# Who makes the rounding additions behind the loop of a cross-attention and feed-forward layer: VectorE or ScalarE

## The chip, the cores and the metric

The kernel runs on one core of one Trainium2 chip. The metric is the device time of one execution in microseconds (us). Three executions of the kernel before took 684.77, 685.49 and 688.87 us; their median, 685.49 us, is the time that the change is set against.

## What is computed

The layer takes 2048 tokens of 256 features. Cross-attention is followed by a feed-forward part with 1024 hidden features, whose two products use weights and activations that are rounded to few levels:

```python
def act_quant(x):
    scale = 127.0 / jnp.clip(jnp.max(jnp.abs(x), axis=-1, keepdims=True), 1e-05)
    return jnp.clip(jnp.round(x * scale), -128, 127) / scale
...
h = bit_linear(x, w1)                  # x rounded by act_quant, w1 to -1, 0, 1
h = depthwise_conv1d(h.transpose(0, 2, 1), conv_w, conv_b)   # three taps along the tokens
h = silu(h.transpose(0, 2, 1))
return bit_linear(h, w2)               # h rounded by act_quant again
```

and outside it `x = x + attention(...)`, then `x = x + feed_forward(layernorm(x))`. So activations are rounded twice: once each block of 128 tokens before the first product, and once the 1024 hidden features of each token before the second. The kernel rounds by adding 12582912 (`MAGIC`) in float32 and taking it away again: behind the first addition only whole numbers fit.

## The kernel before, in words

**The loop.** Attention is done in 8 units (4 stretches of 512 query tokens by 2 pairs of heads), each over all blocks of 128 keys. While units of one stretch run, the feed-forward of earlier tokens is woven in by a plan of calls (`at`, `plan`). Feed-forward works on groups of 256 tokens, `g` = 0 to 7, and in each on 4 slots of 256 hidden features (`NP` = 4): slot `s` belongs to group `s // 4`. Groups 0 to 3 and the first slot of group 4 are computed in the loop, but group 3's rounding and second product are left over.

**Behind the loop** come the last attention rows (four blocks of 128 tokens, `NQB - NSUB` onwards, that is 12 to 15) and 15 slots of groups 4 to 7. Their order is written by hand: `for i in range(N + 4): head(i); tick(i)`, and then one call of `rest` (what group 3 still owes: `scales_spread`, `rounding` of half 0, `rounding` of half 1, and two `end_product`, one for each tick from tick 1 on). Every instruction is kept in program order on its engine, so each engine works through its own list and an instruction that waits holds up all behind it on that engine.

`head(i)`, for i = 1 to 4, finishes block i - 1: normalised tokens `y`, their largest magnitude, the scale `qsc`, then the steps of `quantize` (line 760): `y` times the scale, then the two additions of `MAGIC` in one instruction into the bf16 tile `yq`. TURN (line 765), at the end of a tick, transposes `yq` on TensorE, and ScalarE copies it into `xq_all`.

`tick(i)` (line 1150) moves several slots on by one step each:

- ScalarE: `end_silu` of slot i - 2 (its odd half, from `pre`) and of slot i - 1 (its even half, from the PSUM tile `ph`), lines 904 to 912; both write into the tile `t` of the group.
- VectorE: `dequantize` of slot i (`h` from `ph`, line 822); `output` of products of the tick before (`res`, line 965); `end_last_tap` (line 895).
- ScalarE: `end_taps` of slot i (`pre` and `side`, line 874).
- TensorE: `hidden` of slot i + 1 into one of two `ph` banks (line 811), which the even `end_silu` of slot i - 1 has to have read, then the convolution `end_convolve` of slot i (line 887).

In four of a group's ticks something more is done, at numbers 4, 6, 7 and 8 of the dictionary `at_`: at 4 `magnitudes` of the first four hidden chunks (half 0), at 6 those of half 1, then `columns` and `scales` (the token scales: a transpose, a maximum, a reciprocal, and `cm` on GpSimd); at 7 `scales_spread` (transposes, then ScalarE copies them into `tb`) and `rounding` of half 0; at 8 `rounding` of half 1 and, at the end of the tick, both products `py` of the group. The tick after that is number 5 of the next group, and its `output` calls wait for the products. So a group takes four ticks, and number 8 of one group is number 4 of the next. For the last group, 7, the numbers come one tick later, and its rounding is done in four pieces of 128 tokens at the end.

`rounding(g, i)` (line 945) takes half i of a group (256 tokens by 4 chunks, 1024 elements in each partition): VectorE multiplies `t` by `tb` in place, then makes both additions in one instruction from `t` into the bf16 tile `hq`. The product (line 957) reads all of `hq` as weights: 8 matmuls for each of two blocks of 128 tokens, the first four of each from half 0.

Two buffers matter: `ph` has two banks behind the loop (`ps_h`), and `hq` has one buffer.

Of the kernel before, what the change touches and what calls it, by code (L numbers as in the profile page):

```python
# [10 lines left out]
F32 = mybir.dt.float32  # L11
BF16 = mybir.dt.bfloat16
I32 = mybir.dt.int32
U8 = mybir.dt.uint8
AF = mybir.ActivationFunctionType
ALU = mybir.AluOpType
# [3 lines left out]
P = 128  # L20
FMAX = 3.4028234663852886e38
MAGIC = 12582912.0
# [7 lines left out]
def layer(  # L30
# [22 lines left out]
    nc = tc.nc  # L53

    _, NL, D = x.shape
# [7 lines left out]
    NQB = NL // P  # L63
    G = 256
    QPG = G // P
    NG = NL // G
    QW = 512
    NU = NL // QW
    NSUB = QW // P
# [13 lines left out]
    const = ctx.enter_context(tc.tile_pool(name="const", bufs=1))  # L83
# [9 lines left out]
    ones16 = const.tile([P, P], BF16, name="ones16")  # L93
    nc.vector.memset(ones16, 1.0)

    neg_half = const.tile([P, 2 * H], F32, name="neg_half")
    nc.gpsimd.memset(neg_half, -0.5)

    def inverse_root(x, floor, op, rows, shape, gpsimd=nc.gpsimd):

        gpsimd.tensor_scalar(x, x, floor, None, op)
        e = neg_half[:rows, : shape[-1]] if len(shape) == 1 else neg_half[
            :rows, : shape[0] * shape[1]
        ].rearrange("p (a b) -> p a b", a=shape[0])
        gpsimd.tensor_tensor(x, x, e, ALU.pow)
# [47 lines left out]
    def big(name):  # L153
        return ps_b.tile([P, 2, 512], F32, tag="big", name=name)

    def bank(name, shape, dtype=F32):
        return ps_1.tile(shape, dtype, tag="bank", name=name)
# [16 lines left out]
    tensor, vector = InOrder(nc.tensor), InOrder(nc.vector)  # L174
    scalar, gpsimd = InOrder(nc.scalar), InOrder(nc.gpsimd)
# [108 lines left out]
    with tc.tile_pool(name="pro", bufs=1, side="right") as pro, tc.tile_pool(  # L284
        name="pw", bufs=2, side="right"
# [244 lines left out]
        if NLK == 1:  # L530
            box = {}
# [66 lines left out]
    def quant_scales(amax, n, vector=nc.vector):  # L598

        vector.tensor_scalar(amax, amax, QUANT_EPS, 1.0 / 127.0, ALU.max, ALU.mult)  # L600
        sc = sm.tile([P, QPG], F32, tag="qsc", name="qsc")
        vector.reciprocal(sc[:, :n], amax)
        return sc

    def product_units(amax, i):

        vector.tensor_scalar(amax, amax, w_mean[:, i : i + 1], None, ALU.mult)

    def as_rows(cols, n, by_scalar=False):

        cm = sm.tile([P, QPG, P], F32, tag="cm", name="cm", bufs=3)
        for i in range(n):
            if by_scalar:
                scalar.activation(cm[:, i, :], ones, AF.Copy, scale=cols[:, i : i + 1])
            else:
                gpsimd.tensor_scalar(cm[:, i, :], ones, cols[:, i : i + 1], None, ALU.mult)
        return cm
# [7 lines left out]
    wk = ctx.enter_context(tc.tile_pool(name="wk", bufs=1, side="right"))  # L625
# [3 lines left out]
    with att:  # L629
# [99 lines left out]
        def block_steps(qb, oT, sub, po):  # L729
            box = {}  # L730

            def project_out():
                box["po"] = po()
                for c in range(ND):
                    tensor.matmul(
                        box["po"], oT[:, c, ts(sub, P)], wo_sb[:, c, :],
                        start=(c == 0), stop=(c == ND - 1),
                    )

            def residual():  # L740
                vector.tensor_tensor(x1[qb], box["po"], x1[qb], ALU.add)
                st = sm.tile([P, 6], F32, tag="st3", name="st3")
                box["mv"] = sm.tile([P, 2], F32, tag="mv3", name="mv3")
                vector.bn_stats(st, x1[qb])
                vector.bn_aggr(box["mv"], st)

            def inverse_deviation():
                inverse_root(box["mv"][:, 1:2], LN_EPS, ALU.add, P, (1,), gpsimd)

            def normalize():  # L750
                box["y"] = wk.tile([P, D], F32, tag="y", name="y")
                vector.tensor_scalar(
                    box["y"], x1[qb], box["mv"][:, 0:1], box["mv"][:, 1:2], ALU.subtract, ALU.mult
                )
                vector.tensor_reduce(
                    units1[:, qb : qb + 1], box["y"], AX.X, ALU.max, apply_absolute_value=True
                )
                box["sc"] = quant_scales(units1[:, qb : qb + 1], 1, vector)

            def quantize():  # L760
                vector.tensor_scalar(box["y"], box["y"], box["sc"][:, 0:1], None, ALU.mult)
                box["yq"] = wk.tile([P, D], BF16, tag="yq", name="yq", bufs=2)
                vector.tensor_scalar(box["yq"], box["y"], MAGIC, -MAGIC, ALU.add, ALU.add)

            def transpose():

                t0 = OFF + qb * P
                tp = bank("tpy", [P, 2, P])
                yT = tp[:, 0, :].bitcast(BF16).rearrange("p (c t) -> p c t", c=ND)
                for c in range(ND):  # L770
                    tensor.transpose(yT[:, c, :], box["yq"][:, ts(c, P)], ident16)
                tensor.transpose(tp[:, 1, :], box["cm"][:, 0, :], ident)
                scalar.copy(xq_all[:, :, t0 : t0 + P], yT)
                scalar.copy(ib_all[:, 1 + qb * P : 1 + (qb + 1) * P], tp[:, 1, :])

            def bias():
                gpsimd.tensor_tensor(x1[qb], x1[qb], bo_sb, ALU.add)

            def unit_row():
                product_units(units1[:, qb : qb + 1], 0)  # L780
                box["cm"] = as_rows(units1[:, qb : qb + 1], 1)

            return (
                bias, project_out, residual, inverse_deviation, normalize, quantize, unit_row,
                transpose,
            )
# [12 lines left out]
        for edge in (0, NL + 1):  # L799
# [3 lines left out]
        NC2 = NH // 2  # L803
        groups_ = [{} for _ in range(NG)]
        chunk = {}
        where = {
            "ph": big, "py": lambda: big("py")[:, 0, :D], "later": False,
            "t": lambda: fp.tile([P, G, NC2], F32, tag="t", name="t", bufs=3),
        }
# [135 lines left out]
        def rounding(g, i, tokens=slice(0, G)):  # L945
            b = groups_[g]
            t = b["t"][i][:, tokens, :]
            vector.tensor_tensor(
                t, t, b["tb"][:, tokens].unsqueeze(2).to_broadcast(list(t.shape)), ALU.mult
            )  # L950
            if "hq" not in b:
                b["hq"] = fp.tile([P, G, NH], BF16, tag="hq", name="hq", bufs=1)
            vector.tensor_scalar(
                b["hq"][:, tokens, ts(i, NC2)], t, MAGIC, -MAGIC, ALU.add, ALU.add
            )

        def product(g, i):
            b = groups_[g]
# [23 lines left out]
        def feed_forward(g, k, slots, pace=2):  # L982

            for n in range(slots):
                s, t = g * NP + n, k + n * pace
                for m, call in (
                    (-1, hidden), (-1, dequantize), (0, taps), (1, last_tap), (3, silu),
                ):
                    at(t + m, lambda call=call, s=s: call(s), LATE)
                if n % 2:  # L990
                    at(t + 4, lambda n=n: magnitudes(g, n // 2), LATE)
            if slots < NP:
                return
            t = k + NP * pace
            for m, call in (
                (3, columns), (3, scales), (5, scales_spread), (5, lambda g: rounding(g, 0)),
                (6, lambda g: rounding(g, 1)), (7, lambda g: end_product(g, 0)),
                (7, lambda g: end_product(g, 1)),
            ):
                at(t + m, lambda call=call: call(g), LATE)  # L1000
# [8 lines left out]
        def unit_beat(k):  # L1009

            u, b = divmod(k, NB)
            return (u, b, beats[b]) if u < len(units) else (u, b, [])
# [11 lines left out]
        for k in range(len(units) * NB):  # L1024
            u, b, blocks = unit_beat(k)
            v, _, following = unit_beat(k + 1)
            g, pr = units[u]
# [55 lines left out]
        def y_bank(name):  # L1083
# [5 lines left out]
            later=True,  # L1089
            t=lambda: ptp.tile([P, 2, QW], F32, tag="pt", name="t").rearrange(  # L1090
                "p h q -> p (h q)"
            ).rearrange("p (t c) -> p t c", c=NC2),
# [13 lines left out]
        def po(sub):  # L1106
            if sub % 2 == 0:
                pos[sub // 2] = y_bank("po")
            return pos[sub // 2][:, ts(sub % 2, D)]
# [40 lines left out]
        def tick(i):  # L1150
# [23 lines left out]
            if 7 in at_ and at_[7] != NG - 1:  # L1174
                scales_spread(at_[7])
                rounding(at_[7], 0)
# [76 lines left out]
```

## Time and profile before

The profile is of one execution of 688.55 us. Its traced span is 686.7 us, which leaves 1.85 us around it. The loop ends at about 591 us; the part behind it is what the change touches.

| | before |
|---|---|
| median of three runs | 684.77 / 685.49 / 688.87 us (lowest, median, highest) |
| profiled execution, its span | 688.55 us, 686.7 us |
| mean granted clock of TensorE | 0.972 |
| busy in the span | PE 629.2, VectorE (DVE) 464.1, ScalarE (ACT) 423.8, GpSimd (POOL) 276.6 us |
| 594.5 to 686.8 us, behind the loop | PE 57.67, DVE 74.03, ACT 35.85, POOL 26.78 us of 92.3 us |

The timeline view has a line for each instruction, or for some alike in a row: start, duration, engine, line, operation, tile written and tiles read, sizes, count; in brackets the idle time of the engine just before, and what ended it. All engine calls behind the loop go through a helper at line 170, so lines are told apart by their tiles: `hq<-t` is the rounding of hidden features, `yq<-y` that of a block. A view of stretches gives for each stretch of time the busy time of every engine with the number of instructions, then the granted clock of TensorE (1.00 is full speed), the share of the DMA engines and GB/s. A view of groups adds up instructions of one kind: busy us and mean ns of one, then the idle time before them.

### The profile page before, as it was taken

What the parts mean: (1) busy time and instruction counts of PE and PEld (TensorE: products, weight loads), DVE (VectorE), ACT (ScalarE), POOL (GpSimd) and SP (SyncE); (2) the same over time, 40 slices, a digit from 0 to 9 for tenths busy, and PEclk for the clock granted to TensorE, in tenths of its full rate; (3) what the DMA queues carried; (4) which work ended last, traced back from release to release, by engine and by line L of the source; (5) the groups of instructions that cost most, each with busy time, mean ns of one, the idle gap of its engine ahead of it and who ended that gap; (6) DMA issues with size and microseconds to landing.
All of it is one profiled execution on the core that took longest, in us unless ns stands there. A gap on an engine that the chain in (4) does not pass through costs nothing. (4 is left out here: it accounts for less than half of the span.)

```text
span 686.7 us, 8000 instructions
## 1 busy us (share of the span) xinstructions
PE 629.2 (92%) x2796; PEld 266.3 (39%) x2796; DVE 464.1 (68%) x770; ACT 423.8 (62%) x535; POOL 276.6 (40%) x331
## 2 busy tenths in 40 slices
PE   4999898999999999999999999998899999857754
PEld 2555563333333333333334333332333333345542
DVE  3658774332832766596378779757966797897885
ACT  1656556554556445669945469998765789545540
POOL 2656673221221234244245433425354446742330
PEclk9999999999999999999999999999999999997975
DMA  7600003685878674478849447693564576100001
GB/s 241 170 0 0 1 1 92 128 161 111 167 140 183 128 148 93 93 154 152 185 96 172 101 107 154 125 182 94 107 123 92 132 138 114 31 0 16 16 16 36
DMA packets 32220, 72.12 MB, mean 105 GB/s; under 512 B 7531, under 2 KB 16940, under 8 KB 32172
## 3 DMA queue, kind: packets, MB, share of 16 engines
q0 software_dynamic: 16560, 60.30, 43.3%
q1 hardware_dynamic: 14524, 10.45, 5.1%
q10 hardware_dynamic: 1088, 0.79, 0.4%
q8 instruction: 24, 0.39, 0.2%
q14 instruction: 24, 0.20, 0.1%
HBM read 9.13 MB, written 2.10 MB: 16 GB/s over the span
## 5 line engine op out<-in xcount | busy, mean ns | idle before, releaser
L170 ACT ACTIVATE pt<-st,bias 128x1024 f32<-128x1024 f32 x232 | 242.8, 1112 | 123.1 <-issue 64.6
L170 PE MATMUL st<-q_un,kT 64*128 64x512 f32 x928 | 223.7, 611 | 4.7 <-DVE res L170 1.8
L170 PE MATMUL ot<-pt,v_sb 128*64 128x512 f32 x928 | 216.6, 600 | 0.0
L170 DVE TENSOR_TENSOR vec<-vec,pt 128x1024 f32<-128x1024 f32 x107 | 136.7, 1278 | 40.2 <-ACT pt L170 36.3
L170 PEld LDWEIGHTS st<-q_un,kT 64*128 64x128 f32 x928 | 83.0, 187 | 124.8 <-issue 91.3
L170 PEld LDWEIGHTS ot<-pt,v_sb 128*64 128x64 f32 x928 | 60.2, 136 | 136.7 <-issue 130.4
L170 POOL DMA_DIRECT2D acd<-pt x54 | 44.9, 831 | 127.9 <-ACT pt L170 61.4
L170 POOL DMA_DIRECT2D acc<-pt x61 | 52.7, 865 | 69.4 <-ACT pt L170 51.7
L170 POOL TENSOR_TENSOR pre<-pre,side 128x512 f32<-128x512 f32 (+1 forms) x32 | 38.3, 1196 | 62.3 <-DVE pre L170 51.4
L170 ACT ACT_TABLE_LOAD x34 | 43.6, 1283 | 16.6 <-DMA lb<-in_L_xattn_ln_l_b_dram 7.4
L170 PE MATMUL kv<-wkv_sb,feat 128*128 128x512 f32 (+1 forms) x116 | 52.9, 599 | 0.0
L170 POOL TENSOR_TENSOR ss<-ss,neg_half 128x8 f32<-128x8 f32 (+1 forms) x23 | 39.1, 1702 | 1.9
L170 ACT ACTIVATE t<-pre 128x512 f32<-128x512 f32 (+1 forms) x32 | 29.7, 928 | 11.8 <-POOL pre L170 11.6
L170 POOL TENSOR_SCALAR cm<-ones,units 128x128 f32<-128x128 f32 x16 | 11.8, 739 | 61.4 <-DVE units L170 57.9
L170 DVE COPY oT<-ot 128x512 f32<-128x512 f32 x8 | 5.5, 691 | 44.6 <-PE ot L170 44.6
L170 DVE TENSOR_REDUCE ss<-sq 128x8 f32<-128x512 f32 (+1 forms) x23 | 15.5, 672 | 29.0 <-ACT sq L170 28.9
L170 DVE TENSOR_TENSOR h<-ph,ib_all 128x516 f32<-128x516 f32 x32 | 21.9, 686 | 19.0 <-PE ph L170 18.6
L170 PE MATMUL ph<-h,dg 128*128 128x256 f32 x90 | 25.8, 428 | 7.4 <-DVE h L170 7.4
L170 DVE RECIPROCAL r<-dn 128x512 f32<-128x512 f32 (+1 forms) x11 | 27.3, 2478 | 5.7 <-PE dn L170 5.7
L170 PEld LDWEIGHTS kv<-wkv_sb,feat 128*128 128x128 f32 (+1 forms) x116 | 21.2, 192 | 21.9 <-issue 20.9
L170 ACT ACTIVATE side<-h,cw_sb 128x256 f32<-128x256 f32 x66 | 29.6, 506 | 0.0
L170 PE MATMUL py<-w2T,hq 128*128 128x256 bf16 x128 | 20.8, 317 | 7.2 <-DVE hq L170 7.2
(129 smaller groups left out, 708.9 us busy)
## 6 DMA issues: line engine op xcount, KB each, us to landing
acc<-pt POOLq DMA_DIRECT2D x61, 512.0 KB, 5.1
acd<-pt POOLq DMA_DIRECT2D x54, 512.0 KB, 4.8
tok<-in_x_dram SPq DMA_DIRECT2D x4, 512.0 KB, 6.1
w_sb<-in_L_ffn_w_dram SPq DMA_DIRECT2D x4, 512.0 KB, 5.3
q_un<-in_x_dram SPq DMA_DIRECT2D x4, 512.0 KB, 3.9
out_dram<-res SPq DMA_DIRECT2D x16, 128.0 KB, 1.7
tok<-in_ctx_dram SPq DMA_DIRECT2D x3, 512.0 KB, 4.7
wkv_sb<-in_L_xattn_W_kv_dram ACTq DMA_DIRECT2D x1, 512.0 KB, 7.2
```

The costliest lines, as they stand in the source:

```text
L170: return tc.keep_in_program_order(getattr(self.engine, name)(*args, **kwargs))
```

## The change

Two constants, `MAGIC` and `-MAGIC`, are put into a tile of two columns, and the additions move to ScalarE, each as an activation with the function Identity and one column as its bias. For the last four blocks the multiplication by the scale is taken into the first activation. For hidden features VectorE keeps the multiplication, and the additions of all groups whose rounding stands behind the loop (3, 4, 5 and 6) are made by ScalarE; group 7 and all rounding inside the loop stay as they were. Nothing else is moved: on TensorE, GpSimd and the DMA queues the order of instructions is the same; on ScalarE the new instructions stand where the calls stand.

```diff
+    magic = const.tile([P, 2], F32, name="magic")
+    nc.vector.memset(magic[:, 0:1], MAGIC)
+    nc.vector.memset(magic[:, 1:2], -MAGIC)
...
             def quantize():
+                box["yq"] = wk.tile([P, D], BF16, tag="yq", name="yq", bufs=2)
+                if qb >= NQB - NSUB:
+                    scalar.activation(
+                        box["y"], box["y"], AF.Identity, bias=magic[:, 0:1], scale=box["sc"][:, 0:1]
+                    )
+                    scalar.activation(box["yq"], box["y"], AF.Identity, bias=magic[:, 1:2])
+                    return
                 vector.tensor_scalar(box["y"], box["y"], box["sc"][:, 0:1], None, ALU.mult)
-                box["yq"] = wk.tile([P, D], BF16, tag="yq", name="yq", bufs=2)
                 vector.tensor_scalar(box["yq"], box["y"], MAGIC, -MAGIC, ALU.add, ALU.add)
...
-            vector.tensor_scalar(
-                b["hq"][:, tokens, ts(i, NC2)], t, MAGIC, -MAGIC, ALU.add, ALU.add
-            )
+            hq = b["hq"][:, tokens, ts(i, NC2)]
+            if where["later"] and g < NG - 1:
+                scalar.activation(t, t, AF.Identity, bias=magic[:, 0:1])
+                scalar.activation(hq, t, AF.Identity, bias=magic[:, 1:2])
+            else:
+                vector.tensor_scalar(hq, t, MAGIC, -MAGIC, ALU.add, ALU.add)
```

## The prediction, as it was made before the changed kernel ran

> **What bounds the kernel now.** I read the stretches behind the loop first, cut at the start of one `h` in each group, then the groups of instructions there, and last the timelines of VectorE, ScalarE and TensorE in one group. The stretches:
>
> ```profile
> core 0: us, PE busy (x) PEld busy (x) DVE busy (x) ACT busy (x) POOL busy (x), PEclk, DMA share, GB/s
> 595.30:610.10 14.80, 9.70 (x49) 6.65 (x48) 13.02 (x34) 4.66 (x10) 5.53 (x10) 1.00 0.00 1
> 610.10:623.60 13.50, 6.38 (x29) 4.12 (x28) 12.81 (x30) 5.59 (x13) 5.11 (x8) 0.80 0.00 0
> 623.60:639.10 15.50, 13.41 (x72) 10.54 (x72) 12.43 (x19) 8.87 (x19) 4.94 (x6) 0.85 0.06 18
> 639.10:653.68 14.58, 10.43 (x62) 7.92 (x61) 12.82 (x22) 8.79 (x17) 5.21 (x6) 1.00 0.05 19
> ```
>
> VectorE is busy 12.8 of 14.58 us in the undisturbed group (fourth row), ScalarE 8.8. At first sight VectorE is the bound and ScalarE has 5.8 us to spare. But ScalarE's spare time is not free: it sits in the chain. The timeline of VectorE in that group:
>
> ```profile
> 647.40 1.22 DVE L170 TENSOR_TENSOR t<-t,tb 128x1024 f32<-128x1024 f32 x1 [1.29 <-ACT tb L170]
> 648.66 0.69 DVE L170 TENSOR_SCALAR hq<-t 128x1024 bf16<-128x1024 f32 x1
> 649.27 0.69 DVE L170 TENSOR_TENSOR h<-ph,ib_all 128x516 f32<-128x516 f32 x1
> 649.88 0.47 DVE L170 SCALAR_TENSOR_TENSOR pre<-h,cw_sb,pre 128x256 f32<-128x256 f32 x1
> 650.27 1.22 DVE L170 TENSOR_TENSOR t<-t,tb 128x1024 f32<-128x1024 f32 x1
> 651.52 1.11 DVE L170 TENSOR_SCALAR hq<-t 128x1024 bf16<-128x1024 f32 x1
> 652.55 1.21 DVE L170 TENSOR_REDUCE m<-t 128x256 f32<-128x1024 f32 x1
> 653.68 0.68 DVE L170 TENSOR_TENSOR h<-ph,ib_all 128x516 f32<-128x516 f32 x1
> 654.28 0.86 DVE L170 SCALAR_TENSOR_TENSOR res<-py,am,q_un 128x256 f32<-128x256 f32 x2
> ```
>
> From the first multiplication of `t` to the end of both `res` VectorE runs without a wait, 7.66 us (the next instruction starts at 655.06). ScalarE and TensorE beside it:
>
> ```profile
> 647.27 0.68 ACT L170 ACTIVATE t<-pre 128x256 f32<-128x256 f32 x1
> 648.67 0.73 ACT L170 ACTIVATE t<-ph,cb_sb 128x256 f32<-128x256 f32 x1 [0.72 <-PE ph L170]
> ```
>
> ```profile
> 649.44 0.60 PE L170 MATMUL ph<-xq_all,w1T 128*128 128x258 bf16 x4 [0.82 <-ACT t L170]
> 650.02 1.56 PE L170 MATMUL ph<-h,dg 128*128 128x256 f32 x6
> 651.41 0.60 PE L170 MATMUL py<-w2T,hq 128*128 128x256 bf16 x4
> 652.69 1.53 PE L170 MATMUL py<-w2T,hq 128*128 128x256 bf16 x12 [0.67 <-DVE hq L170]
> ```
>
> The reader is to see who waits for whom: the even silu (`t<-ph`) frees a bank for `hidden`; `hidden` gives the next `h`; the last 12 matmuls of `py` start when the second `hq` is there; `res` needs them. Now they are just done before VectorE comes to them.
>
> **What leaves VectorE.** Eight `hq` of 1024 elements take 0.61 or 1.02 us each until the next instruction starts (648.66 to 649.27, 651.52 to 652.55), four of each kind: about 6.5 us. Four blocks shed `y` times scale and `yq`, 602.81 to 603.41 = 0.60 each: 2.4 us. In all 8.9 us of 74. Two memsets of one column join VectorE at the start, near the row `second` (0.06 us), while it waits 4.33 us for the first tokens: nothing.
>
> **What ScalarE gets.** Sixteen activations of 1024 and eight of 256 elements. The trace has no Identity of 1024; the nearest row is the exponential of the same size with a bias column:
>
> ```profile
> L170 ACT ACTIVATE pt<-st,bias 128x1024 f32<-128x1024 f32 x232 | 242.8, 1112 | 123.1 <-issue 64.6
> ```
>
> and, of the groups behind the loop, two of 256 elements and the instruction that is replaced:
>
> ```profile
> L170 ACT ACTIVATE pre<-h,cb_sb,cw_sb 128x256 f32<-128x256 f32 x15 | 8.8, 588 | 20.1 <-DVE h L170 20.1
> L170 ACT ACTIVATE side<-h,cw_sb 128x256 f32<-128x256 f32 x15 | 7.4, 495 | 0.0
> L170 DVE TENSOR_SCALAR hq<-t 128x1024 bf16<-128x1024 f32 x8 | 7.2, 898 | 0.3
> ```
>
> By length the exponential is nearest: I take 1.11 us, with 0.95 as the lower end (a tile in SBUF with one column less) and 1.30 as the upper (silu writes `t` with gaps and takes 0.68 where `side` takes 0.49, so the gaps in `hq` might add 0.19). The second activation needs the first's result, so nothing overlaps: 1.11 + 0.04 + 1.11 = 2.26 us a pair, against 0.69 to 1.10 for one instruction before. The 256-wide pair is `pre`'s 0.60 plus `side`'s 0.49. No table load is added: Identity (`pre`) and Silu alternate behind the loop, and the last load there stands at 590.56.
>
> Here a rule speaks against the change: the Trainium skill, "ScalarE: Activation LUTs", section "Rules for kernel authors", puts plain additions on VectorE, not on ScalarE. The row agrees in price (2.26 against about 0.9), but price alone would make the change good or bad by which engine has time: by busy sums the group would have VectorE 12.8 - 1.6 = 11.2 and ScalarE 8.8 + 4.5 = 13.3 us, both under 14.58, so a gain would still be possible. What decides is the order.
>
> **One group in order, from the first multiplication at 0.** VectorE: `t` 0 to 1.22, `h` 1.15, `pre` 1.76, second `t` 2.15 to 3.37, `m` 3.30 to 4.43, then `h` of the next slot. ScalarE: first pair 1.28 to 3.54. Behind it on ScalarE stand both silus of the next tick: they start at 3.45 and 3.91, the even one ends 4.62 (before: 649.40 - 647.40 = 2.00). So `hidden` starts at 4.68 (before 2.04) and ends 5.28: VectorE waits for it 0.9 us. ScalarE's `pre` and `side` follow to 5.28, then the second pair, whose multiplication has been ready since 3.37: 5.28 to 7.54. Then the last 12 matmuls of `py`: 7.60 to 9.13, and `res` to 9.57, against 7.66: **+1.9 us** a group. VectorE saves 1.6 us and waits 3.5 for `h` and `res`. What follows to the next multiplication (7.84 us of `pre`, `h`, `m`, scales, `cm`, `tb`) is unchanged. Groups 4 and 5 pay this in full: +3.8.
>
> **Group 6** has no `hidden` behind it. Pairs 1.28 to 3.54 and, after two silus, 4.53 to 6.79. `py` starts 6.85 after the first multiplication (before: 668.70 - 662.90 = 5.80), and the last silu, now behind the pair, ends 7.37, so that `m` comes later too, still covered by `py`: +1.1.
>
> **The four blocks and group 3.** From tick 2 to tick 3 ScalarE and TensorE hold each other in a ring: two copies 0.43, the pair 2.17 (its end overlaps the next by 0.09), `y` 0.64, `yq` 0.40, silus 0.46 and 0.70, `hidden` 0.44, convolution 1.30, transposes 0.55, three handovers 0.12 to 0.18: 7.2 us a tick, where VectorE's tick takes 6.25 and 6.04 now (`h` at 610.10, 616.35, 622.39). VectorE gets ahead by its savings at first. The first pair can begin between 612.0 and 613.2 (the copies end at 613.18 now, and move up by what VectorE saved, at most 1.2); the second 7.2 later; pair, `y`, `yq`, two silus and `hidden` more put `h` at 624.3 to 625.5, against 623.60: +0.7 to +1.9, I take +1.2.
>
> **The clock.** In the new order TensorE is idle from the end of a convolution (648.63, 1.23 on the scale above) to `hidden` at 4.68: 3.4 us, where it was 0.82. The trace shows what little work does: after 3.9 idle us in the 4.5 before 617.07 the clock fell, and the convolution of 1.46 us took 2.93 at 623.12 (granted clock 0.80 in that stretch). The skill, "TensorE: Matmul & The Clock Gate", Part 1, says that half speed comes after an idle window of about 3.4 us, and windows run freely. By the trace alone (a gap of 2.03 at 641.4 cost nothing) I would add 0; with the rule and a halved clock, convolution and `py` behind the gap take 1.4 and 1.25 longer and all of it is on the path: +2.8 a group. I take half, for groups 4 and 5: +2.8. In the first stretch the clock had fallen already: nothing.
>
> **Sum**: 1.2 + 3.8 + 1.1 + 2.8 = +8.9 us on the profiled 688.55, giving 697.4. The median of the runs is 3.1 lower than that execution; on it the same sum gives 685.49 + 8.9 = **694.4**.
>
> **Rivals.** (a) *VectorE's relief counts*: 8.9 us of work leave the busiest engine and ScalarE absorbs it, 676.6 us. For it: 12.8 of 14.58 busy. Against: `hidden` waits 0.82 us for ScalarE already, and `py` 0.67 us for `hq`. It would need the group's four activations 1.9 us shorter together, so about 0.64 us each instead of 1.11; at 1.11 it is lost. No row of that size is under 1.1. Chance 0.05. (b) *Mechanism right, clock stays*: +6.1 or less, 688 to 692.3 us; for it: gaps of 2 us were harmless; against: 3.4 is longer. Chance 0.29. (c) *As forecast, with at least some of the clock*: above 692.3. Chance 0.66. (d) Inside (c): the clock halves in both groups and the writes with gaps cost 0.19 more on every pass: 6.1 + 0.7 + 2.7 + 5.6 = +15, 700.6 us.
>
> **How the numbers follow.** Low end: passes of 0.95 save 0.64 in each of three groups (1.9), the first stretch costs 0.7, no clock: 6.1 - 1.9 - 0.5 = +3.7, less a little for the unknown: 688. High end is (d): 700.5. Outside remain 0.05 for (a) below, and about as much for more above. A measurement of this kernel can tell about 1% from no change, 6.85 us: faster means under 678.6, slower over 692.3.
>
> **What would show it.** Right: `res` and `h` of VectorE idle some 2.3 and 0.9 us for `py` and `ph` in groups 4 and 5; the last `py` matmuls released by ScalarE's `hq`; passes of 1.1 us; the time between first multiplications of groups 16.4 us instead of 14.6; VectorE's busy time 9 us less in a longer end. Wrong: VectorE still without waits from `t` to `res`; passes under 0.7 us; TensorE's clock at 1.00 after gaps of 3.4 us would take away the last 2.8 us.

## The result, and the profile after

The changed kernel takes 695.9 us (median of 6 runs, 694.29 to 697.59), the kernel before 686.2 us (6 runs in all, 684.77 to 688.87). The ratio is 1.0131, with a 95% interval of 1.0116 to 1.0146: slower by 1.3%, about 9.0 us. The forecast was 8.9 us more, 694.4 us on the median of the first three runs, in a range of 688.0 to 700.5.

The profiled execution has a span of 693.9 us against 686.7. The part in front of the last attention rows happened to be 1.6 us shorter in it, so I compare from the first reciprocal `r` behind the loop (595.38 before, 593.79 after). All stages below are of one profiled execution each; the end of the loop is untouched.

| from the first `r`, us | before | after |
|---|---|---|
| to the first multiplication `t<-t,tb` of group 4 | 37.06 | 41.12 |
| from there to that of group 6 (groups 4 and 5) | 30.46 | 34.13 |
| from there to the scales `am` of group 7 | 9.04 | 10.01 |
| from there to the last `res` | 9.95 | 9.95 |
| sum | 86.51 | 95.21 |

So 8.70 us were lost behind the loop: 4.06 at the start, 3.67 in groups 4 and 5, 0.97 in group 6. The stretches of the changed kernel, cut at the same `h` as those of before:

```profile
core 0: us, PE busy (x) PEld busy (x) DVE busy (x) ACT busy (x) POOL busy (x), PEclk, DMA share, GB/s
608.13:627.22 19.09, 8.71 (x31) 6.36 (x31) 10.42 (x24) 12.54 (x24) 5.83 (x9) 0.59 0.00 0
627.22:640.63 13.41, 9.19 (x54) 7.61 (x54) 10.33 (x18) 9.18 (x18) 5.18 (x5) 0.88 0.06 21
640.63:657.69 17.06, 11.34 (x61) 8.89 (x61) 11.47 (x19) 12.44 (x22) 5.19 (x6) 0.90 0.05 16
```

No engine is full now. In the third row VectorE (DVE) works 11.5 of 17.06 us and ScalarE (ACT) 12.4, where VectorE had 12.8 of 14.58. The first row was 13.50 us long at a granted clock of 0.80; it is 19.09 long at 0.59. The timeline of VectorE in group 5, from the first multiplication:

```profile
651.99 1.22 DVE L174 TENSOR_TENSOR t<-t,tb 128x1024 f32<-128x1024 f32 x1 [1.21 <-ACT tb L174]
653.13 0.69 DVE L174 TENSOR_TENSOR h<-ph,ib_all 128x516 f32<-128x516 f32 x1
653.73 0.48 DVE L174 SCALAR_TENSOR_TENSOR pre<-h,cw_sb,pre 128x256 f32<-128x256 f32 x1
654.13 1.22 DVE L174 TENSOR_TENSOR t<-t,tb 128x1024 f32<-128x1024 f32 x1
655.26 1.21 DVE L174 TENSOR_REDUCE m<-t 128x256 f32<-128x1024 f32 x1
657.69 0.69 DVE L174 TENSOR_TENSOR h<-ph,ib_all 128x516 f32<-128x516 f32 x1 [1.22 <-PE ph L174]
660.84 0.48 DVE L174 SCALAR_TENSOR_TENSOR res<-py,am,q_un 128x256 f32<-128x256 f32 x1 [2.45 <-PE py L174]
661.72 0.48 DVE L174 SCALAR_TENSOR_TENSOR res<-py,am,q_un 128x256 f32<-128x256 f32 x1 [0.39 <-PE py L174]
```

Both `hq` are gone from it, and in their place stand three waits, 4.06 us in all (by chance the same figure as the loss at the start). ScalarE in the same time:

```profile
653.24 1.15 ACT L174 ACTIVATE t<-t,magic 128x1024 f32<-128x1024 f32 x1 [1.29 <-DVE t L174]
654.42 1.15 ACT L174 ACTIVATE hq<-t,magic 128x1024 bf16<-128x1024 f32 x1
655.48 0.64 ACT L174 ACTIVATE t<-pre 128x256 f32<-128x256 f32 x1
655.92 0.66 ACT L174 ACTIVATE t<-ph,cb_sb 128x256 f32<-128x256 f32 x1
...
657.25 1.13 ACT L174 ACTIVATE t<-t,magic 128x1024 f32<-128x1024 f32 x1
658.41 1.15 ACT L174 ACTIVATE hq<-t,magic 128x1024 bf16<-128x1024 f32 x1
```

ScalarE sits idle for 1.29 us until the multiplication is done, with the odd silu (`t<-pre`) ready behind the pair. The even silu (`t<-ph`) starts 3.93 us after the first multiplication; before, it was 1.27. TensorE (PE) behind it:

```profile
651.82 1.46 PE L174 MATMUL ph<-h,dg 128*128 128x256 f32 x6
656.64 1.02 PE L174 MATMUL ph<-xq_all,w1T 128*128 128x258 bf16 x4 [3.36 <-ACT t L174]
657.45 2.48 PE L174 MATMUL ph<-h,dg 128*128 128x256 f32 x6
659.77 1.91 PE L174 MATMUL py<-w2T,hq 128*128 128x256 bf16 x16
```

`hidden` waits 3.36 us for the silu, and what follows the gap runs at half speed: 1.02 instead of 0.60, 2.48 instead of 1.46. At the start of the stretch, with blocks and group 3, the same happens with longer gaps. VectorE waits 7.87 us there:

```profile
627.22 0.70 DVE L174 TENSOR_TENSOR h<-ph,ib_all 128x516 f32<-128x516 f32 x1 [7.87 <-PE ph L174]
```

This `h` comes 33.43 us after the first `r`; before, it came 28.22 after it, without a wait. TensorE in front of it, in the first of two such ticks:

```profile
612.03 0.28 PE L174 MATMUL tpy<-ident,cm 128*128 128x128 f32 x1
617.21 1.02 PE L174 MATMUL ph<-xq_all,w1T 128*128 128x258 bf16 x4 [4.90 <-ACT t L174]
618.02 2.76 PE L174 MATMUL ph<-h,dg 128*128 128x256 f32 x6
620.58 0.42 PE L174 MATMUL tpy<-ident,yq 128*128 128x128 bf16 x2
```

### The profile page after: what moved, and what is told of

Its sections match the earlier page's. It is cut to its first block, busy times and chain, and to the rows that moved or that the text cites. A ratio compares the mean times of both kernels' runs of the same rounds, so it can differ in the third digit from the quotient of the medians.

```text
span 693.9 us, 8010 instructions
## 1 busy us (share of the span) xinstructions
PE 628.4 (91%) x2796; PEld 267.7 (39%) x2796; DVE 455.9 (66%) x756; ACT 442.9 (64%) x559; POOL 277.5 (40%) x331
## 5 line engine op out<-in xcount | busy, mean ns | idle before, releaser
L174 PE MATMUL ph<-xq_all,w1T 128*128 128x258 bf16 x128 | 21.5, 295 | 21.6 <-ACT t L174 20.7
L174 PE MATMUL ph<-h,dg 128*128 128x256 f32 x90 | 27.3, 450 | 1.5 <-DVE h L174 1.5
```

The costliest lines, as they stand in the source:

```text
L174: return tc.keep_in_program_order(getattr(self.engine, name)(*args, **kwargs))
```

## The experiments

The theory: the pairs of activations hold up silus, `hidden` and `py` by their place and length in ScalarE's list, and the gaps that this leaves on TensorE cost clock on top. Rivals: the loss follows the amount of work put on ScalarE; the clock has no part in it; any handover away from VectorE costs. Each kernel below was timed in five rounds beside the kernel before.

**Blocks alone.** Condition in `rounding` never true.

```diff
-            if where["later"] and g < NG - 1:
+            if where["later"] and g < 0:
```

> Only the last four blocks round on ScalarE, the hidden features of all groups stay on VectorE. If the loss comes from the pairs of 1024-wide activations standing in front of the silus and the products, this part is harmless: VectorE sheds 0.60 us in each of four blocks and ScalarE's list of a tick (7.2 us with a pair, 5.0 without) stays under VectorE's 6.1, so about 1 to 2 us faster than before, near 684.5. If each part costs in proportion to the work put on ScalarE (4.4 of 22.7 us), about 2 us slower than before, near 688.

Measured: ratio 1.001 (0.9999 to 1.002), median 687.91 us. Both expectations missed: no gain, and no 2 us of loss either. Stages: 37.68, 30.66, 9.04 and 9.74. VectorE gets ahead (`h` of slots 18 to 21 come up to 1.6 us earlier than before), but the next `h` comes 28.95 us behind the first `r`, against 28.22: its bank waits for TensorE and ScalarE. What VectorE saved is lost again there. TensorE's lines point to the same order of ScalarE's list:

```profile
616.69 1.02 PE L174 MATMUL ph<-xq_all,w1T 128*128 128x258 bf16 x4 [4.08 <-ACT t L174]
617.50 2.77 PE L174 MATMUL ph<-h,dg 128*128 128x256 f32 x6
```

The activations of a block stand in front of the silus too. `hidden` waits 4.08 and 2.67 us in two ticks (before: 1.66 and 1.67), and the convolution behind it takes 2.77 us both times (before: 1.90 and 2.93). From `y` to `y` ScalarE's tick takes 6.68 us (614.48 to 621.16), where the expectation had 5.0 and VectorE's has 6.1.

**Hidden features alone.** Condition in `quantize` never true.

```diff
-                if qb >= NQB - NSUB:
+                if qb >= NQB:
```

> Only the hidden features of groups 3 to 6 round on ScalarE, the four blocks stay on VectorE. If the pairs are the cause, all of the loss remains but for some 1 us in each tick of the ring of group 3 (y and yq leave it): 694 to 696. If the blocks' part carries much of the loss at the start of the stretch, where the change lost 4.1 us up to group 4, about 692.

Measured: ratio 1.0094 (1.0078 to 1.011), median 693.37: below the 694 to 696 that was expected if the pairs alone are the cause, above the 692 of the other case. Stages: 37.58, 34.12, 10.02 and 9.94. The loss of groups 4, 5 and 6 (34.12 and 10.02) is the changed kernel's to 0.01 us: it belongs to the pairs. But at the start blocks alone cost 0.62 us, pairs alone 0.52, and both together 4.06. They do not add up, which needed a run of its own. The stages of three single profiles make the excess 2.9 us; the ratios of all runs make it smaller, 1.0131 against 1.001 and 1.0094, 0.0027 or about 1.9 us.

**Group 3 back on VectorE**, all else as changed.

```diff
-            if where["later"] and g < NG - 1:
+            if where["later"] and 3 < g < NG - 1:
```

> The changed kernel with group 3 back on VectorE; the blocks and groups 4 to 6 stay on ScalarE. At the start of the stretch blocks alone cost +0.6 us up to the first multiplication of group 4, hidden features alone +0.5, both together +4.1. If these 4.1 us come from a ring in ScalarE's list that is only longer than VectorE's tick when it holds both y and yq and a pair, the start costs +0.6 again and the groups keep their 4.6: +5.2 us in all, ratio 1.007 to 1.009. If the start's loss has another cause, it stays: 1.012 to 1.014.

Measured: ratio 1.0067 (1.0047 to 1.0088), median 692.52, just under the expected figures. The start takes 37.55 us, +0.49: the loss there needs `y`, `yq` and a pair of group 3 in one tick of ScalarE's list. Groups 4 and 5 took 35.06 in this execution, 0.9 more than in the changed kernel with the same instructions there, which shows how much a single profile can differ in the stages with gaps.

**Dummy matmuls in the gaps.** All work of the changed kernel, and 12 matmuls that nobody reads in front of `hidden` in four ticks.

```diff
+            if i in (3, 4, 7, 11):
+                warm(12)     # 12 x matmul(bank, ones16, w1T[:, 0, :512])
             if i + 1 < N:
                 hidden(slots[i + 1])
```

> The changed kernel with 12 extra matmuls of 128x512 in bf16, whose result nobody reads, put in front of hidden in the four ticks where TensorE now waits 3.4 to 4.9 us for ScalarE. They fit into the gap (2.6 us at full clock). If the clock that falls in these gaps is part of the loss, hidden takes 0.60 and the convolution 1.46 us again, the two ticks of group 3 shrink from 8.9 to about 7.3 us and the whole gains about 3 us on the changed kernel: 692 to 693.5. If the clock has no part in the loss, it stays at 696 or gets worse by what the extra matmuls delay.

Measured: ratio 1.0056 (1.0036 to 1.0075), median 691.02. The mean granted clock is 0.989 against 0.968 in the profiled executions, and 0.982 to 0.989 against 0.968 to 0.971 over all. More work for TensorE made the kernel 0.75% faster than the changed one, about 5 us, more than the 3 expected. Stages: 36.49, 33.19, 9.99 and 9.93. TensorE's timeline at the start (the trace lacks one record of the 12):

```profile
611.76 2.75 PE L174 MATMUL warm<-w1T,ones 128*128 128x512 bf16 x11 [0.63 <-ACT ib_all L174]
616.04 0.60 PE L174 MATMUL ph<-xq_all,w1T 128*128 128x258 bf16 x4 [1.53 <-ACT t L174]
616.48 1.46 PE L174 MATMUL ph<-h,dg 128*128 128x256 f32 x6
```

`hidden` and the convolution are back at 0.60 and 1.46 us. From pair to pair ScalarE's tick is 7.04 us here (611.59 to 618.63), where it is 8.90 in the changed kernel (612.77 to 621.67). The whole 4.06 us of the start are gone, with 0.57 to spare; of the 3.67 in groups 4 and 5, 0.94 are.

Not all of this is the work of the dummies. At the start the two profiles differ by 4.63 us, and 1.46 of them lie in front of the first dummy matmul (the first pair starts 18.98 us after the first `r` in the changed kernel, 17.52 here). Up to there TensorE has the same work at the same times, and yet `hidden` runs at two speeds, the changed kernel first:

```profile
608.72 1.02 PE L174 MATMUL ph<-xq_all,w1T 128*128 128x258 bf16 x4 [1.65 <-ACT t L174]
609.00 0.60 PE L174 MATMUL ph<-xq_all,w1T 128*128 128x258 bf16 x4 [1.65 <-ACT t L174]
```

The profile of the changed kernel thus holds a slow stretch that its order of work does not force; which of its other executions have it is not recorded. From the first pair on, the dummies gave back 3.17 us at the start and 0.94 in groups 4 and 5, 4.1 in all. VectorE in group 5, first multiplication at 647.15, shows what is left with the clock kept up:

```profile
652.45 0.69 DVE L174 TENSOR_TENSOR h<-ph,ib_all 128x516 f32<-128x516 f32 x1 [0.81 <-PE ph L174]
655.50 0.48 DVE L174 SCALAR_TENSOR_TENSOR res<-py,am,q_un 128x256 f32<-128x256 f32 x1 [2.35 <-PE py L174]
656.37 0.48 DVE L174 SCALAR_TENSOR_TENSOR res<-py,am,q_un 128x256 f32<-128x256 f32 x1 [0.39 <-PE py L174]
```

The next instruction starts 9.62 us after the first multiplication (10.13 in the changed kernel, 7.66 before).

**Pairs behind the silus.** The same work, but the pairs of group 3 and of half 0 of groups 4 to 6 are kept in a list `owed` and issued in the next tick, after `end_silu`.

```diff
+            if where["later"] and g < NG - 1 and (i == 0 or g == 3):
+                owed.append(additions)     # both activations
...
             if 0 <= i - 1 < N:
                 end_silu(slots[i - 1], 0)
+            while owed:
+                owed.pop(0)()
```

> The changed kernel with the same work on ScalarE, but the pairs of group 3 and those of half 0 of groups 4 to 6 are issued one tick later, behind both silus. If order decides, the ring of group 3 loses its pair (8.9 to about 6.5 us a tick) and most of the 4.1 us lost there comes back; in groups 4 and 5 the 1.2 us wait of h goes, but half 1 is rounded at the same time as now, so the wait of res grows by as much: 691.5 to 693. If the load on ScalarE decides, wherever it stands: 696.

Measured: ratio 1.0058 (1.0042 to 1.0073), median 690.65, a little better than expected. Stages: 35.96, 35.82, 9.55 and 9.50. The start is 1.1 us better than before the change; groups 4 and 5 are 1.7 worse than in the changed kernel. TensorE in group 5 shows why:

```profile
649.46 0.60 PE L174 MATMUL ph<-xq_all,w1T 128*128 128x258 bf16 x4 [0.81 <-ACT t L174]
649.89 1.46 PE L174 MATMUL ph<-h,dg 128*128 128x256 f32 x6
651.54 0.66 PE L174 MATMUL py<-w2T,hq 128*128 128x256 bf16 x4 [0.19 <-ACT hq L174]
654.65 2.78 PE L174 MATMUL py<-w2T,hq 128*128 128x256 bf16 x12 [2.45 <-ACT hq L174]
```

`hidden` is on time again. The gap has moved behind the first four `py`, and now the last 12, on which both `res` wait, run at half speed: 2.78 us instead of 1.53. So the wait was not only moved, as expected, but became dearer.

**One pass instead of two**, with the blocks on VectorE.

```diff
-                scalar.activation(t, t, AF.Identity, bias=magic[:, 0:1])
-                scalar.activation(hq, t, AF.Identity, bias=magic[:, 1:2])
+                scalar.activation(hq, t, AF.Identity, bias=magic[:, 0:1])
```

> The blocks stay on VectorE, and of the pair on ScalarE only one activation is left: it adds the constant and writes hq, and the second addition is left out, so hq does not hold the rounded values. Place and waits are those of the changed kernel, the price on ScalarE is half: 2.3 us less in a group. The prediction put the break-even at 1.9 us less in a group. If that holds, the groups take as long as before and the whole is within 0.2% of it: ratio 0.998 to 1.003. If the handover and not the length costs, most of the 6.5 us stay: ratio above 1.006.

Measured: ratio 0.9972 (0.9962 to 0.9982), median 685.65: at the break-even and a little past it, just under the expected range. Stages: 35.84, 30.65, 8.34 and 9.94; groups 4 and 5 together take as long as before the change (30.46). VectorE's waits in group 5:

```profile
648.96 0.68 DVE L174 TENSOR_TENSOR h<-ph,ib_all 128x516 f32<-128x516 f32 x1
650.85 0.48 DVE L174 SCALAR_TENSOR_TENSOR res<-py,am,q_un 128x256 f32<-128x256 f32 x1 [1.21 <-PE py L174]
651.73 0.48 DVE L174 SCALAR_TENSOR_TENSOR res<-py,am,q_un 128x256 f32<-128x256 f32 x1 [0.39 <-PE py L174]
```

1.60 us of waits take what the two `hq` had, 1.64, and the group takes 14.49 us. In group 4 `py` ran at half speed (3.04 us for 16 matmuls), and it takes 16.16; before, the two took 14.96 and 15.50, with a slow stretch at the end of the second. So the close agreement of the two sums is partly chance, but the loss of the changed kernel is gone. The handover itself is not what costs; its length and place are.

**One half each**: blocks on VectorE; ScalarE makes half 0, one tick later, behind the silus; VectorE makes half 1.

```diff
-            if where["later"] and g < NG - 1:
+            if where["later"] and g < NG - 1 and i == 0:
...
+                owed.append(additions)     # both activations, issued behind end_silu
             else:
                 vector.tensor_scalar(hq, t, MAGIC, -MAGIC, ALU.add, ALU.add)
```

> The blocks stay on VectorE. Of groups 3 to 6 ScalarE rounds half 0 only, one tick later, behind both silus; VectorE rounds half 1 itself. If what counts is when hidden and the last py matmuls can start, hidden is as early as before, hq of half 0 is ready at about 4.3 us after the first multiplication, that of half 1 at 4.4, and both res come by about 6.1: VectorE runs without a wait and keeps the 0.61 us of one instruction in each group: 1.5 to 2.5 us faster than before, ratio 0.997. If any additions on ScalarE cost the kernel time, slower than before by about half of the hidden part's 6.5 us: ratio 1.005.

Measured: ratio 0.9932 (0.9919 to 0.9946), median 683.02 us, faster than both kernels: 0.68% under the one before, 4.7 us, twice what was expected. Stages: 36.35, 28.29, 7.72 and 9.94. VectorE and TensorE in group 5, first multiplication at 646.16:

```profile
651.72 0.68 DVE L174 TENSOR_TENSOR h<-ph,ib_all 128x516 f32<-128x516 f32 x1
652.32 0.86 DVE L174 SCALAR_TENSOR_TENSOR res<-py,am,q_un 128x256 f32<-128x256 f32 x2
```

```profile
648.19 0.60 PE L174 MATMUL ph<-xq_all,w1T 128*128 128x258 bf16 x4 [0.81 <-ACT t L174]
648.63 1.46 PE L174 MATMUL ph<-h,dg 128*128 128x256 f32 x6
650.28 1.97 PE L174 MATMUL py<-w2T,hq 128*128 128x256 bf16 x16 [0.19 <-ACT hq L174]
```

No wait stands in front of `h` or `res`, and TensorE's gaps in these lines are 0.81 and 0.19 us. VectorE keeps 0.72 us in this stretch (`res` end at 6.94 instead of 7.66). Of the gain 2.17 us lie in groups 4 and 5 and 1.32 in group 6. That is more than VectorE's share. Part of the surplus is clock that the kernel before lost in its profiled execution, in front of group 6:

```profile
658.72 2.37 PE L170 MATMUL ph<-h,dg 128*128 128x256 f32 x6
662.90 1.23 DVE L170 TENSOR_TENSOR t<-t,tb 128x1024 f32<-128x1024 f32 x1 [2.21 <-ACT tb L170]
```

With one half on each engine this convolution takes 1.46 us (656.76). The wait for `tb` was 1.29 in front of group 5, so about 0.9 us of the 2.17 is this; and in group 6 the last 12 `py` take 2.13 instead of 2.78. Both are estimates from single executions; the ratio is over all runs.

**The same with half 0 in front of the silus.** The cut is set against the changed kernel, with the blocks on VectorE.

```diff
-            if where["later"] and g < NG - 1:
+            if where["later"] and g < NG - 1 and i == 0:
```

> The one-half-each kernel (its ratio was 0.993) with one thing put back: the pair of half 0 stands where the changed kernel has it, in front of the silus of the next tick. The work of every engine is the same. If the place decides, hidden starts 4.7 instead of 2.0 us after the first multiplication, convolution and all 16 py come behind it, and the second res ends at about 8.7 us at full clock, 1 to 2 us more if TensorE falls to half speed in its gap of 3.4 us, where it ends before 7 in the one-half-each kernel: groups 4 and 5 lose 2 to 3 us each, ratio 0.999 to 1.003. If the amount of work on ScalarE decides: 0.993 again.

Measured: ratio 1.0031 (1.0021 to 1.004), median 689.6, at the upper end of what was expected. Stages: 35.74, 34.25, 8.32 and 9.81. Same instructions, other place: 1% of the whole, nearly all in groups 4 and 5 (34.25 against 28.29).

```profile
652.98 1.02 PE L174 MATMUL ph<-xq_all,w1T 128*128 128x258 bf16 x4 [3.45 <-ACT t L174]
653.79 2.52 PE L174 MATMUL ph<-h,dg 128*128 128x256 f32 x6
656.15 1.91 PE L174 MATMUL py<-w2T,hq 128*128 128x256 bf16 x16
```

Here `py` has had both halves of `hq` for 3.3 us and waits for the convolution alone, so the slow clock costs in full. The amount of work on ScalarE is refuted as the cause: the same amount is 0.7% faster than before in one place and 0.3% slower in the other.

**Additions on GpSimd (POOL)**, blocks on VectorE.

```diff
-                scalar.activation(t, t, AF.Identity, bias=magic[:, 0:1])
-                scalar.activation(hq, t, AF.Identity, bias=magic[:, 1:2])
+                gpsimd.tensor_scalar(hq, t, MAGIC, -MAGIC, ALU.add, ALU.add)
```

> The blocks stay on VectorE. The additions of groups 3 to 6 are made by GpSimd, in one instruction of two additions as VectorE makes them; VectorE sheds the same 6.5 us as in the changed kernel, and ScalarE's list is as before. If the loss comes from ScalarE's list, which holds silus and so hidden and h, the waits of h for ph go, and the result hangs on the length of GpSimd's instruction only: at 1.2 to 2.2 us half 1 is ready 4.7 to 5.6 us after the first multiplication and res does not wait: ratio 0.995 to 1.001. If taking the additions from VectorE to any engine costs the same handover, ratio 1.005 to 1.01.

Measured: ratio 1.0165 (1.015 to 1.018), median 699.53: a miss, and the condition that it hung on is the reason. Stages: 36.06, 39.25, 12.66 and 9.89. The instruction takes over three times VectorE's worst (1.10):

```profile
651.97 3.65 POOL L174 TENSOR_SCALAR hq<-t 128x1024 bf16<-128x1024 f32 x1 [1.71 <-DVE t L174]
656.30 3.62 POOL L174 TENSOR_SCALAR hq<-t 128x1024 bf16<-128x1024 f32 x1
```

Two of them and a `pre` between them end 9.7 us after the first multiplication in group 4 and 9.4 in group 5, and `res` waits (4.55 us at 641.52, 4.93 at 661.09). `h` in front of it does not wait (636.30 follows 635.17 at once), so that part of the expectation held. The run says nothing on a helper engine that is fast enough.

## Why the prediction was right, and where its terms were not

- **What moves** was right: behind the loop VectorE's busy time fell from 74.03 to 65.49 us (8.5, forecast 8.9), and ScalarE's rose from 35.85 to 54.95.
- **The price of a pass** was right: 1.11 was taken from the exponential, the group of `hq<-t,magic` has a mean of 1.148 and `t<-t,magic` 1.142 us. The lower end of 0.95 was put down for one column less than the exponential has, but the pass has one column (`magic`) as the exponential has (`bias`). The 0.19 for writing with gaps did not appear: both have the same length, though only one writes with gaps.
- **The order in a group** was right. Worked out: silu pair from 3.45, `hidden` at 4.68, second pair 5.28 to 7.54, `py` at 7.60, `res` to 9.57. In group 5 of the trace: 3.49, 4.65, 5.26 to 7.57, 7.78, and 10.13. With the clock kept up by dummy matmuls the end is at 9.62, and the waits are 0.81 for `h` and 2.35 and 0.39 for `res`, where 0.9 and 2.3 were put down for the first two. The last 12 `py` are released by ScalarE's `hq` there, as forecast; in the changed kernel all 16 come behind the slow convolution.
- **The clock term was wrong in two places, in opposite directions.** The step "convolution and `py` behind the gap take 1.4 and 1.25 longer and all of it is on the path: +2.8 a group" failed; the prediction took half of it (and 1.4 and 1.25 make 2.65, not 2.8). The convolution did take 2.48 us, 1.02 longer, but behind the gap the second pair on ScalarE lasts until 7.57 anyway. At 7.78 `py` started, with the clock back: 16 matmuls in 1.91 us, where the last 12 alone were to take 1.53. That is 0.18 and 0.38, 0.56 us a group. The dummy matmuls gave back 0.94 in both groups, where 2.8 had been put down.
- **The base of a group was disturbed too.** The prediction set 16.4 us from first to first multiplication against 14.6. Measured were 17.08 and 17.05, but the profile before has 14.96 and 15.50: a first multiplication of 1.62 instead of 1.22 us in group 4, and the slow convolution near 659 in group 5. The 7.84 us that were to stay unchanged hold that slow stretch; in the changed kernel they are 6.92. So groups 4 and 5 lost 3.67 us where 3.8 + 2.8 = 6.6 was forecast.
- The step "**In the first stretch the clock had fallen already: nothing**" failed the other way. Before, the slow matmuls there lay beside VectorE's own work (12.81 of 13.50 us busy). In the changed kernel they are part of ScalarE's ring, and a tick grows from 7.2, the sum in the prediction (its terms make 7.09 before the handovers; 7.04 was measured with the clock kept up), to 8.90. The clock fell further as well, from 0.80 to 0.59 in that stretch. So 4.06 us were lost at the start instead of 1.2: a cost that was hidden came onto the path and grew.
- **Sum.** 2.9 us too much in groups 4 and 5 and 2.9 too little at the start cancel. That the sum came out at 8.9 against 9.0 is luck; that it lies in the range is not, since the order alone was put at 6.1. Keeping TensorE busy takes the ratio from 1.0131 to 1.0056, about 5 of the 9 us (3.4 to 6.8 by both intervals). So more comes back with the clock kept up than the 2.8 us forecast for it, and most of that at the start. Whether clock or order is the larger part is not shown: the start then is 0.57 us shorter than before, so the dummies also remove clock loss that the kernel before has, and the kernel before was not run with dummies.
- **Group 6** was +1.1, measured +0.97, in the order forecast: pairs from 1.26 and 4.43 us (worked out: 1.28 and 4.53), `py` at 6.77 (6.85).
- **The rival on the other side**, that VectorE's relief counts, is right for another order: its break-even of 1.9 us less a group fits the run with half the passes (2.3 less a group, groups 4 and 5 together as long as before). With one half on each engine and behind the silus, the relief comes through.

What stays open: that blocks alone gain nothing because of `hidden` and the slow convolution was read from one timeline and not tried with dummies. How the half-speed stretches fall differs between executions, so that stage times of single profiles hold to about 1 to 1.5 us.

## What to carry to other kernels

Busy sums said that ScalarE had room for the additions, and it had; but on an in-order engine that feeds another stage it counted where an instruction stands and how long it holds up what is behind it, not how much the engine does in all. Before work is moved to such an engine, write down what is queued behind it and who waits for that, and put it behind the instructions that release others. A slow-clock stretch that is covered by other work today can come onto the path when the cover goes: work out the ring (the instructions of two engines that wait for each other in turn) at both clocks.

## What the hardware showed that was not expected

- After a gap of 3.4 to 4.9 us TensorE ran `hidden` in 1.02 instead of 0.60 us and the convolution in 2.48 to 2.76 instead of 1.46; 2.75 us of useless matmuls in such a gap prevented it. After a gap of 2.45 us (pairs behind the silus) 12 `py` also took 2.78 instead of 1.53. The gap in front alone does not decide it: after one of 1.65 us with the same work before it `hidden` took 1.02 in the profile of the changed kernel and 0.60 in that of the dummy run.
- GpSimd takes 3.62 to 3.65 us for two additions of 128x1024 from float32 to bf16, VectorE 0.69 to 1.10, ScalarE 2.3 for its two passes.
